# Storing full slots in 128 pieces of 16 KB instead of 256 pieces of 8 KB

## The chip, the cores and the metric

The kernel runs on one core of a Trainium2 chip. Times are microseconds on the device, from the first to the last thing that the program does there. Data come from the chip's main memory (HBM) into the on-chip memory (SBUF, 128 partitions) and go back by DMA; 16 DMA engines serve the core.

## The reference

There are 128 matrices `x[b]` of 128 x 1024 numbers (float32), eight weight matrices of 128 x 128, and one index per matrix.

```python
def _L0_cond_ref(x, subjects, weights):
    w = weights[subjects]
    out = jnp.einsum('bct,bcd->bdt', x, w)
    return out
x = x + _L0_cond_ref(x, itok_B_0_7, L0_cond_weights)
```

So every matrix is multiplied by the weight matrix that its index selects, and the product is added to it. Input and output are 67.1 MB each.

## The kernel before, in words

Four matrices (`H * G` = 2 x 2) make a slot: 16 KB in each of the 128 partitions, 2 MB in all. There are 32 slots of work (`NT`) and twelve places for them in SBUF (`SLOTS`); work slot i uses place i % 12. A half is two matrices (h = 0 or 1).

ScalarE's DMA queue issues the loads, one per matrix, 512 KB each (`load`, L137): 32 runs of 16 KB in HBM, four rows of the matrix to a run, into 4 KB in each of 128 partitions, one row to a partition. Slots 0 to 10 are loaded without a wait but for the weight copies that stand at slot 6 in ScalarE's program (L220 to L231); slot 11 waits until the weights have been turned (L233), since its place is used for that. From slot 12 on, ScalarE waits at L235 until slot i - 12 has been stored.

GpSimd waits for each slot's four loads (L240 to L244) and passes the word on to TensorE through `s_ready`. TensorE (`multiply`, L169) waits at L170 for the weights of the half, at L171 for the slot, and multiplies into PSUM at L175. VectorE (`add`, L184) waits for the product, adds it in place at L187 and copies the weights for the next slot (`place`, L164, L166).

SyncE's DMA queue loads the indices (L193) and the weight matrices, in 32 runs of 16 KB (L195), and then issues the stores (`store`, L145). It first waits until slot 7 has been loaded (L246, `AHEAD` = 8) and then, slot by slot, until the second half has been added (L250, `s_added`). Slots 0 to 30 are stored whole, by one DMA of 2 MB each: these are the full slots. Slot 31 is stored in a first half of 1 MB, then one matrix of 512 KB, then the last matrix by L279. When a store has landed, its place is free and ScalarE may issue the loads of the slot 12 further on. Nothing in this is decided by a scheduler: the order in each queue is the order of the code.

In SBUF a full slot is one run of 16 KB in each partition. In HBM its rows lie in four matrices, 4 KB in each. `store` cuts the SBUF side into pieces of `g` matrices:

```python
out[b + q0 : b + q1].rearrange("g d t -> d g t"),
xs[i % SLOTS][:, q0:q1, :].rearrange("d (o g) t -> d o (g t)", g=min(G, q1 - q0)),
```

Of the kernel before, what the change touches and what calls it, by code (L numbers as in the profile page):

```python
# [30 lines left out]
G = 2  # L31
# [4 lines left out]
SLOTS = 12  # L36
# [19 lines left out]
def transfer(nc, engine, out, in_):  # L56

    later, nc._always_lower_symbolic_ap = nc._always_lower_symbolic_ap, False  # L60
    ins, outs = engine.lower_ap_dma(in_), engine.lower_ap_dma(out)
    nc._always_lower_symbolic_ap = later
    return engine.add_instruction(
        mybir.InstDMACopy(
            name=nc.get_next_instruction_name(),
            engine=engine.engine,
            ins=ins,
            outs=outs,
            mode="Copy",
            cce_op=ALU.bypass,  # L70
            queue=QUEUES[engine.engine],
        )
    )
# [3 lines left out]
def kernel(  # L77
# [17 lines left out]
    if room:  # L95
        sbuf("room", C, room // 4)
    x_all = sbuf("x_all", C, SLOTS * H * G * T)
    xs = [
        x_all[:, i * H * G * T : (i + 1) * H * G * T].rearrange("c (q t) -> c q t", t=T)
        for i in range(SLOTS)  # L100
    ]
# [43 lines left out]
    def store(i, q0, q1):  # L145
        b = i * H * G
        transfer(
            nc,
            nc.sync,
            out[b + q0 : b + q1].rearrange("g d t -> d g t"),  # L150
            xs[i % SLOTS][:, q0:q1, :].rearrange("d (o g) t -> d o (g t)", g=min(G, q1 - q0)),
        ).then_inc(s_slot[i % SLOTS], DMA)

    def subjects_of(i):
# [36 lines left out]
    with tc.tile_critical():  # L191
# [55 lines left out]
        for i in range(NT):  # L247
            for h in range(H):
                if i == NT - 1 or h == H - 1:
                    nc.sync.wait_ge(s_added, i * H + h + 1)  # L250
                    store(i, h * G if i == NT - 1 else 0, (h + 1) * G - (i * H + h == NT * H - 1))
# [62 lines left out]
```

## Time and profile before

| | |
|---|---|
| median of 3 runs | 324.44 us (324.38 to 324.48) |
| the profiled execution | 323.93 us, its span 322.2 us |
| DMA | 134.76 MB in 15,059 packets, 418 GB/s over the span |
| PE busy | 239.5 us (74%) |
| VectorE busy | 168.2 us (52%) |
| stores of 2 MB | 31, median 44.9 us from issue to landing |
| loads of 512 KB | 128, median 10.6 us from issue to landing |

PE is TensorE's matmuls, DVE is VectorE, ACT ScalarE, POOL GpSimd, SP SyncE. q10 is ScalarE's DMA queue and q1 SyncE's. A DMA packet in these views is one piece of a transfer, or one of the small packets of 4 bytes that count a transfer's arrival, one per engine and transfer. A row of the windows gives the stretch, its length, busy time and instructions of PE, PE's weight loads, DVE, ACT and POOL, then the granted TensorE clock, the share of the 16 DMA engines and GB/s. A row of the waits gives who waited for whom: total, times, longest, in us.

### The profile page before, as it was taken

The page shows a single profiled execution, that of the slowest core. Times are in us where ns is not written, and L with a number is a line of the kernel's source. Part 1 is how long each engine was busy: PE and PEld are TensorE (multiplying, and loading weights), DVE is VectorE, ACT ScalarE, POOL GpSimd, SP SyncE. Part 2 cuts the span into 40 slices and gives each one's busy share as a digit, 9 for nine tenths or more (in the row PEclk, how much of TensorE's full clock was granted, in tenths as well). Part 3 has the DMA queues.
Part 4 walks back from the last instruction along what each step waited for, and adds up shares of the span by engine and source line. Part 5 has one row for each costly group of instructions (what it writes and reads, how often), then busy time and mean ns, then how long its engine had stood idle before and what let it go on. Part 6 is the DMA issues. An engine that isn't in the chain of part 4 may idle for free. (4 is left out here: it accounts for less than half of the span.)

```text
span 322.2 us, 2399 instructions
## 1 busy us (share of the span) xinstructions
PE 239.5 (74%) x518; PEld 99.4 (31%) x518; DVE 168.2 (52%) x204; ACT 11.1 (3%) x17; POOL 0.2 (0%) x4
## 2 busy tenths in 40 slices
PE   5001999999999999999999999996959779300000
PEld 2000344444444444444444444432423234000000
DVE  3002367767776776677677667763754707500000
ACT  0094000000000000000000000000000000000000
POOL 0000000000000000000000000000000000000000
PEclk9555799999999999999999999997998959755555
DMA  7999999999999999999999999999999999999996
GB/s 291 425 423 427 429 410 410 438 420 419 431 432 428 417 422 425 430 423 425 429 423 426 427 431 422 424 429 436 427 411 425 437 415 427 426 425 426 426 429 279
DMA packets 15059, 134.76 MB, mean 418 GB/s; under 512 B 2609, under 2 KB 2610, under 8 KB 2866
## 3 DMA queue, kind: packets, MB, share of 16 engines
q1 hardware_dynamic: 8914, 67.64, 49.9%
q10 hardware_dynamic: 6144, 67.12, 49.6%
q14 instruction: 1, 0.01, 0.0%
HBM read 67.63 MB, written 67.11 MB: 418 GB/s over the span
## 5 line engine op out<-in xcount | busy, mean ns | idle before, releaser
L175 PE MATMUL ps<-x_all,w 128*128 x512 | 234.8, 617 | 35.2 <-DVE w L166 24.6
L187 DVE TENSOR_TENSOR x_all<-ps,x_all 128x2048 f32 x64 | 146.7, 2292 | 84.6 <-DVEq L186 84.6
L175 PEld LDWEIGHTS ps<-x_all,w 128*128 128x128 f32 x512 | 97.6, 196 | 172.4 <-issue 171.5
L166 DVE COPY w<-w_runs 128x128 f32 x132 | 23.2, 219 | 0.8 <-DVE w_runs L262 0.8
L262 DVE STREAM_TRANSPOSE w_runs<-x_all 128x1024 f32<-128x1024 f32 x1 | 1.2, 1245 | 21.0 <-ACT x_all L224 21.0
L224 ACT COPY x_all<-x_all 32x256 f32<-32x256 f32 x16 | 9.8, 614 | 0.4
L205 PE MATMUL ps<-zeros 128*128 128x512 f32 x6 | 4.7, 952 | 1.7 <-DVE zeros L202 1.7
L205 PEld LDWEIGHTS ps<-zeros 128*128 128x128 f32 x6 | 1.8, 325 | 3.7 <-issue 2.1
L260 DVE STREAM_TRANSPOSE x_all<-w_runs 128x1024 f32<-128x1024 f32 x1 | 1.2, 1245 | 2.8 <-DMA w_runs<-in_L_cond_weights_dram 2.8
L224 ACT ACT_TABLE_LOAD x1 | 1.3, 1283 | 16.6 <-issue 16.6
L202 DVE MEMSET zeros<- 128x512 f32 x1 | 0.5, 485 | 1.0 <-SPq L191 1.0
L214 DVE TENSOR_SCALAR near<-given 1x128 int32<-1x128 int32 x1 | 0.2, 215 | 0.6 <-DMA given<-in_itok_B_dram 0.6
L218 DVE CUSTOM_DVE_ANT_0 index<-near,wrap 1x256 uint16<-1x256 uint16 x1 | 0.3, 278 | 0.0
L216 DVE TENSOR_SCALAR wrap<-near 1x128 int32<-1x128 int32 x1 | 0.2, 216 | 0.0
L301 POOL MEMSET const-bfloat16-1.0<- 128x1 bf16 x1 | 0.1, 101 | 0.0
L301 POOL MEMSET const-uint8-127<- 128x1 uint8 x1 | 0.1, 101 | 0.0
L301 POOL MEMSET const-float32-0.0<- 128x1 f32 x1 | 0.1, 98 | 0.2 <-issue 0.2
L301 POOL MEMSET const-float32-1.0<- 128x1 f32 x1 | 0.1, 98 | 0.0
L301 DVE BASE_LOAD x1 | 0.0, 21 | 0.1
L212 DVE MEMSET index<- 1x4 int32 x1 | 0.1, 62 | 0.0
## 6 DMA issues: line engine op xcount, KB each, us to landing
x_all<-in_x_dram ACTq DMA_DIRECT2D x128, 512.0 KB, 10.6
out_dram<-x_all SPq DMA_DIRECT2D x31, 2048.0 KB, 44.9
out_dram<-x_all SPq DMA_DIRECT2D x1, 1024.0 KB, 25.9
out_dram<-x_all SPq DMA_DIRECT2D x2, 512.0 KB, 21.2
w_runs<-in_L_cond_weights_dram SPq DMA_DIRECT2D x1, 512.0 KB, 4.4
given<-in_itok_B_dram SPq DMA_DIRECT2D x1, 0.5 KB
```

Source lines behind the costliest of these rows:

```text
L166: copy = nc.vector.tensor_copy(ws[q], w_all[:, bass.ds(subject[q], 1), :])
L175: mm = nc.tensor.matmul(ps[h][:, q % G, t : t + N], ws[q][:, 0, :], x_all[:, bass.ds(at, N)], start=True, stop=True,)
L187: nc.vector.tensor_tensor(mine, ps[h].rearrange("d g t -> d (g t)"), mine, ALU.add).then_inc(s_added, 1)
L202: nc.vector.memset(zeros, 0.0).then_inc(s_zeros, 1)
L205: nc.tensor.matmul(ps[P_SLOTS - 1][:, G - 1, :N], zeros[:, :D], zeros, start=True, stop=True)
L214: nc.vector.tensor_scalar(near, given, -S, S - 1, ALU.max, ALU.min).then_inc(s_index, 1)
L216: nc.vector.tensor_scalar(wrap, near, 0, S, ALU.is_lt, ALU.mult).then_inc(s_index, 1)
L218: nc.vector.tensor_tensor(index[:, :B], near, wrap, ALU.add).then_inc(s_index, 1)
L224: nc.scalar.copy(w_moved[b * BLOCK : (b + 1) * BLOCK, :].rearrange("l (a m h k j) -> l a h m k j", a=BLOCKS, m=PER, j=RUN, k=BLOCK // RUN) ...
L260: nc.vector.transpose(w_turned, w_runs).then_inc(s_wall, 1)
L262: nc.vector.transpose(w_runs, w_moved).then_inc(s_wall, 1)
L301: nc = _bacc.Bacc("TRN2", target_bir_lowering=False, num_devices=1)
```

## The change

Where a store covers four matrices, the SBUF side is handed over as one piece of 16 KB in each partition (`g` = 4) instead of two of 8 KB (`g` = 2). Stores of two matrices or of one keep their form. The bytes, the order of the code and all waits stay the same, and so do the instructions on every engine.

```diff
     def store(i, q0, q1):
         b = i * H * G
         transfer(
             nc,
             nc.sync,
             out[b + q0 : b + q1].rearrange("g d t -> d g t"),
-            xs[i % SLOTS][:, q0:q1, :].rearrange("d (o g) t -> d o (g t)", g=min(G, q1 - q0)),
+            xs[i % SLOTS][:, q0:q1, :].rearrange("d (o g) t -> d o (g t)", g=q1 - q0),
         ).then_inc(s_slot[i % SLOTS], DMA)
```

## The prediction, made before the changed kernel ran

> **What bounds the kernel now.** I read the page's strips first, then the windows, then the DMA view cut to two stretches, then the waits. In the page's strip the DMA engines are busy in every slice:
>
> ```profile
> DMA  7999999999999999999999999999999999999996
> DMA packets 15059, 134.76 MB, mean 418 GB/s; under 512 B 2609, under 2 KB 2610, under 8 KB 2866
> ...
> q1 hardware_dynamic: 8914, 67.64, 49.9%
> q10 hardware_dynamic: 6144, 67.12, 49.6%
> ```
>
> q10 is ScalarE's queue (128 loads), q1 SyncE's (stores, weights, indices). The two shares add to 99.5% of 16 engines' span, so the end is set by bytes over 427 GB/s. The packet counts are pieces plus 16 small count packets of 4 B for each DMA: a load is 32 pieces of 16 KB, on one engine two pieces and one count (128 x 48 = 6144); a full store is 256 pieces of 8 KB, on one engine sixteen and a count.
>
> The windows show what lies behind PE: it is done by 280 us, and 40 us of pure storing follow.
>
> ```profile
> 272.00:280.00 8.00, 4.36 (x11) 1.60 (x9) 5.23 (x7) 0.00 (x0) 0.00 (x0) 0.91 1.01 426
> 280.00:288.00 8.00, 0.00 (x0) 0.00 (x0) 0.00 (x0) 0.00 (x0) 0.00 (x0) 0.50 1.01 426
> ...
> 304.00:312.00 8.00, 0.00 (x0) 0.00 (x0) 0.00 (x0) 0.00 (x0) 0.00 (x0) 0.50 1.01 427
> ```
>
> So today the last slot's loading, matmuls and adds are covered by a backlog of some ten slots of stores. That cover is what the change touches. The DMA view for 50 to 100 us, where both queues hold work, shows how they share:
>
> ```profile
> q10 hardware_dynamic: 1136, 12.34, 58.3%
> q1 hardware_dynamic: 1162, 9.00, 42.6%
> ```
>
> Packet numbers are equal, bytes are not: an engine takes one packet from one queue, then one from the other. The trace's packet records of one engine read load, store, load, store, count, store, over and over. Last, who waits on PE:
>
> ```profile
> PE ps L175 <- PEq L171: 10.5, 3, 4.0
> ```
>
> PE lacked a loaded slot three times only (near 217, 236 and 256 us).
>
> **Part 1: fewer packets.** 31 stores lose 128 pieces each: 3968 packets, so q1 has 4946. In the packet records an 8 KB store piece takes 310.7 ns and a 16 KB load piece 616; 4 KB takes 159. The line through the store sizes gives 614 for 16 KB. Two small pieces cost 621.4, one large one 614 to 616: 5.4 to 7.4 ns saved 3968 times over 16 engines, 1.3 to 1.8 us. The other bound is the rate: loads alone run at 428 GB/s (10 to 40 us), stores alone at 426 (268 to 312), and half a per cent of the stores' 152 us is 0.7. I take 1.4, the packet price, because it is for the same byte count on the same engines. It counts only while the engines stay full.
>
> **Part 2: the shares.** Turns stay one for one, but a store turn now carries 16 KB. Before, the 17 turns of a store on an engine go with 17 load turns, 5.67 loads: 2.97 + 2.10 MB in 11.9 us, a loaded slot every 8.4 us. The trace confirms it: slots 9 to 12 are complete at 58.8, 67.1, 75.5 and 84.1 us. After, a store has 9 turns, beside 3 loads: 1.57 + 2.10 MB in 8.6 us. A slot is stored every 8.6 us and loaded every 11.5 us while both queues hold work.
>
> [...]
>
> **Part 3: where that leads.** All up to the first store packet at 48.6 us stays. PE and DVE take 7.05 us a slot (adds of one half start at 101.1 and 108.2), so slot i starts at 36 + 7.05 i as long as it is there. Slot 8 is there at about 50.5 and slot i at 50.5 + 11.5 (i - 8). These meet at slot 17, 158 us. From there PE waits at L171 for every slot, 4 us each; DVE, SP's waits for s_added and the stores behind them on SP follow.
>
> A slot's last add ends 10 us after its last load (0.35 to start, 7.05 matmuls, 2.3 add, small gaps), and about 2 us more pass before its store can move. Stores could begin at 48.6 + 8.6 i; the data are ready at 50.5 + 11.5 (i - 8) + 12. These meet at slot 27, about 280 us. Then the store queue runs dry, where before it held ten slots.
>
> How late is the last load? The engines are full until then. Most of them finish everything at 319.5 us before, so 318.1 with the 1.4 saved. A slot's store takes 4.87 us of all engines. If n slots have been stored when the last load ends, that is at 318.1 - 4.87 (32 - n). Slot 30 cannot be among them: it lands less than 12 us ahead of slot 31. Slot 29 is ready some 8 us ahead and takes its turns against the last loads. So n is between 29 and 30: 303.5 to 308.4 us. I take 29.8, 307.4, since a store with every second turn is through in 8.6 us.
>
> From there nothing covers the chain: landing 0.5, start 0.35, matmuls 7.05, add 2.3, issue 0.1, first packet about 2 (an uncontended first load needed 1.3, the first store under load 4.5), two 512 KB stores at 16 pieces x 159 ns = 2.5, end of program 1.4 (322.15 less 320.75). That is 16.2. If the clock drops, 1.7 more: after the waits at 217 and 236 us the next two slots took 15.88 us instead of 14.1, at a granted clock of 0.5 for 3.4 us. The wait ahead of slot 31 is 2 to 4 us, like those, so I count 1.4 of it. Span: 307.4 + 16.2 + 1.4 = 325.0.
>
> **Sum.** The profiled execution took 323.93 us, span 322.2 and 1.7 around it. New: 325.0 + 1.7 = 326.7, 2.8 more. The median of the runs shown is 324.44, 0.5 above the profiled one, so 327.2. Hidden at no cost: PE's waits in the middle (14 slots x 4 us), because the engines have queued loads throughout; if that cover failed each would show. The code's other orders, and DVE, ACT and POOL instructions, do not change.
>
> **Rivals.**
> First, *the chain stays covered*. If n is near 29, the last load ends at 303.5 and the chain without a clock drop at 319.7, when the engines are still busy with slot 30; then only the saving shows: 324.4 - 1.4 = 323.0. For it: 5 us, one slot's store, decide, and loads get every turn that a dry store queue leaves; it wins where the last load ends before 304.5. Against: slot 29 is ready too early to leave its turns unused. The same time comes out if turns are whole groups of pieces, so that the shares do not move: against it stand the equal packet numbers. Together 0.21. [...]
> Second, *cancelled*: last load near 305.5 without a drop, span within 0.6 us of today's: 324.4, chance 0.06.
> Third, *pieces are cut* on the way, at the 4 KB rows of the output, and nothing moves: 324.4. Against: loads with 4 KB rows on the on-chip side appear as 16 KB packets. Chance 0.03.
> Fourth, *worse*: stores of slot 30 also get in ahead of the last loads, or slot 31 meets two windows of half clock (one wait of 4.0 us before cost 2.9): last load at 309.5, chain 19.5, span 329: 331. Chance 0.09.
> My forecast keeps 0.61.
>
> **Numbers.** What a measurement of this kernel can tell from no change is about 0.2%, 0.65 us. Faster is the first rival, 0.21. Same: the second and third, 0.09. Slower: the forecast and the fourth, 0.70. The range goes from the covered case, 322.9, to 330.0, short of the fourth rival; the forecast's own range is 325.5 to 329.
>
> **What would show it.** q1 at 4946 packets; in the window 50 to 100 us equal packet numbers but about 8.5 MB loaded to 12.8 MB stored; slots loaded every 11.5 us; PE waiting at L171 from 160 us on some 14 times; last matmul near 316 instead of 276; DMA gaps and less than full rate in the last 10 us. It is wrong if loads keep 58%, if the last load ends before 304 us, or if 16 KB store pieces are far from 615 ns.

## The result, and the profile after

The changed kernel takes 326.08 us (median of 22 runs), the kernel before 324.10 us in runs beside it. The ratio is 1.0056, with a 95% interval of 1.0032 to 1.0079, about 1.8 us slower. One of the 22 runs, of 329.69 us, lies more than 1.5% above the shortest and is left out of the comparison. The kernel has also become uneven: 324.02 to 328.44 us over the other 21 runs, where nearly all runs of the kernel before lie between 323.6 and 324.7. The execution that was profiled is one of the long ones: 328.25 us, span 326.5.

The page of the changed kernel, the DMA strip, packets and queues:

```profile
DMA  7999999999999999999999999999999999999956
...
DMA packets 11091, 134.76 MB, mean 413 GB/s; under 512 B 2609, under 2 KB 2610, under 8 KB 2866
...
q10 hardware_dynamic: 6144, 67.12, 49.0%
q1 hardware_dynamic: 4946, 67.64, 48.8%
```

The 3968 packets are gone. What is new is the 5 in the strip's last slices: the engines run short of work near the end. The DMA view of the changed kernel for 50 to 100 us, the same stretch as before:

```profile
q1 hardware_dynamic: 829, 12.27, 57.7%
q10 hardware_dynamic: 838, 9.09, 43.0%
```

Packets are again one for one, and now the stores have the larger share of the bytes. So the loads fall behind. The timeline of PE in the changed kernel (start, time, instructions, and in brackets the idle time ahead and what ended it) shows the place, and the waits show its total:

```profile
154.98 7.13 PE L175 MATMUL ps<-x_all,w 128*128 x16 [0.64 <-PEq L171]
166.66 8.83 PE L175 MATMUL ps<-x_all,w 128*128 x16 [4.55 <-PEq L171]
178.32 7.13 PE L175 MATMUL ps<-x_all,w 128*128 x16 [2.84 <-DVE w L166]
...
298.28 7.13 PE L175 MATMUL ps<-x_all,w 128*128 x16 [1.51 <-PEq L171]
309.94 8.82 PE L175 MATMUL ps<-x_all,w 128*128 x16 [4.53 <-PEq L171]
```

```profile
PE ps L175 <- DVE w L166: 38.6, 6, 24.2
PE ps L175 <- PEq L171: 29.1, 10, 4.5
```

From 155 us on PE takes one slot at a time and then waits. Rows that name DVE's weight copy belong to the same wait: at 178 us the copy for that half had long been done (at 174.9 us), and GpSimd's record says that the slot was complete at 177.97 us. The row at 309.94 is the last slot. The last time in GpSimd's view of L244 is the moment at which slot 31 is complete. The kernel before, and below it the changed kernel, 42 us later:

```profile
L244 POOLq EVENT_SEMAPHORE  x31: 17/17/17, 14.6 to 267.5; - x31
```

```profile
L244 POOLq EVENT_SEMAPHORE  x31: 17/17/17, 14.7 to 309.6; - x31
```

What that does to the end is seen in the windows of the changed kernel (last two columns: DMA share and GB/s):

```profile
304.00:312.00 8.00, 3.47 (x7) 1.31 (x6) 3.40 (x6) 0.00 (x0) 0.00 (x0) 0.90 1.00 426
312.00:316.00 4.00, 4.00 (x8) 1.63 (x7) 0.36 (x1) 0.00 (x0) 0.00 (x0) 0.77 0.66 279
316.00:318.00 2.00, 2.00 (x6) 0.95 (x5) 2.00 (x3) 0.00 (x0) 0.00 (x0) 1.00 0.00 0
318.00:320.00 2.00, 0.77 (x2) 0.00 (x0) 1.19 (x3) 0.00 (x0) 0.00 (x0) 1.00 0.46 197
```

The store of slot 30 is through at 315.9 us by the packet records, and then the engines have nothing to do but wait for slot 31's matmuls and adds.

### The profile page after: what moved, and what is told of

It is laid out like the page before. It is cut to its first block, busy times and chain, and to the rows that moved or that the text cites. A ratio compares the mean times of both kernels' runs of the same rounds, so it can differ in the third digit from the quotient of the medians.

```text
span 326.5 us, 2399 instructions
## 1 busy us (share of the span) xinstructions
PE 249.4 (76%) x518; PEld 102.7 (31%) x518; DVE 168.2 (52%) x204; ACT 11.1 (3%) x17; POOL 0.2 (0%) x4
## 3 DMA queue, kind: packets, MB, share of 16 engines
q1 hardware_dynamic: 4946, 67.64, 48.8%
## 5 line engine op out<-in xcount | busy, mean ns | idle before, releaser
L175 PE MATMUL ps<-x_all,w 128*128 x512 | 244.1, 635 | 67.7 <-DVE w L166 38.6
L175 PEld LDWEIGHTS ps<-x_all,w 128*128 128x128 f32 x512 | 100.8, 202 | 211.6 <-issue 211.0
L166 DVE COPY w<-w_runs 128x128 f32 x132 | 23.2, 218 | 0.8 <-DVE w_runs L262 0.8
## 6 DMA issues: line engine op xcount, KB each, us to landing
x_all<-in_x_dram ACTq DMA_DIRECT2D x128, 512.0 KB, 40.3
out_dram<-x_all SPq DMA_DIRECT2D x31, 2048.0 KB, 25.6
```

Of the source, the lines that this page charges most:

```text
L166: copy = nc.vector.tensor_copy(ws[q], w_all[:, bass.ds(subject[q], 1), :])
L175: mm = nc.tensor.matmul(ps[h][:, q % G, t : t + N], ws[q][:, 0, :], x_all[:, bass.ds(at, N)], start=True, stop=True,)
```

## The experiments

The theory is the one of the prediction: the engines take one piece from each queue in turn, as the 829 packets beside 838 above have it, so a piece's size sets its queue's share; with 16 KB store pieces the loads come late, and past a certain point the last slot's chain (load, matmuls, add, store) has no stores left to hide behind. The rival is that a 16 KB store piece is itself what costs. "Last slot" in the table further down is GpSimd's record of the moment at which slot 31 is complete. Each edit is shown against the changed kernel; e3 makes its edit in the kernel before.

**e5: the same pieces, with a head start for the loads.**

```diff
-AHEAD = 8
+AHEAD = 10
```

> The changed kernel, with its first store let go when slot 9 is loaded instead of slot 7 (AHEAD = 10); pieces as in the changed kernel. Turns theory: loads start the shared part two slots further ahead and the stores some 10 us later, the last slot is loaded near 302 us and is covered or nearly so: within 1.5 us below or 0.5 above the kernel before, 322.8 to 324.6. Rival (the piece itself costs): stays near 326.

324.00 us against 323.90, ratio 1.0004 (0.9995 to 1.0013). All 31 full stores have 16 KB pieces and q1 has 57.7% of the engines' time between 60 and 110 us, as in the changed kernel, yet nothing is lost. PE's last slot begins at 303 us, and the windows of e5 show the engines at full rate until the usual end:

```profile
q1 hardware_dynamic: 845, 12.27, 57.7%
```

```profile
303.37 8.56 PE L175 MATMUL ps<-x_all,w 128*128 x16 [2.66 <-PEq L171]
```

```profile
312.00:318.00 6.00, 0.00 (x0) 0.00 (x0) 2.56 (x3) 0.00 (x0) 0.00 (x0) 0.88 0.97 409
```

PE waits nearly as long in e5 as in the changed kernel (28.8 us at L171 and 33.1 put down to L166, beside 29.1 and 38.6). So neither the piece nor PE's waits cost anything by themselves that these runs can tell. The rival falls here.

**e8: half that head start.**

```diff
-AHEAD = 8
+AHEAD = 9
```

> The changed kernel with AHEAD = 9: its first store waits for slot 8 instead of slot 7, half as much as the run with AHEAD = 10. Turns theory: what decides is whether the store of slot 29 or 30 still moves ahead of the last load; with this start the phase falls on the late side, the last slot is loaded near 308 to 309.5 us and the end is 2.5 to 4.5 us above the kernel before, 326.4 to 328.4. Rival (a head start of the loads is worth the same for each slot): half of what AHEAD = 10 gives back, near 325.

327.08 us against 323.75, ratio 1.0087 (1.0068 to 1.0105): a slot more of head start makes it no better than the changed kernel, as the turns theory had it, by which the stores that still move ahead of the last load decide. In the packet records, store pieces worth 29.7 slots have begun in e8 when the last load ends, as in the changed kernel's first execution, and 28.5 in e5. The rival asked for 325 us. The last slot is complete at 309.55 us.

```profile
309.90 8.82 PE L175 MATMUL ps<-x_all,w 128*128 x16 [2.07 <-PEq L171]
```

**e2 and e7: the large pieces early only, or late only.**

```diff
-            xs[i % SLOTS][:, q0:q1, :].rearrange("d (o g) t -> d o (g t)", g=q1 - q0),
+            xs[i % SLOTS][:, q0:q1, :].rearrange("d (o g) t -> d o (g t)", g=q1 - q0 if i < 24 else min(G, q1 - q0)),   # e2
+            xs[i % SLOTS][:, q0:q1, :].rearrange("d (o g) t -> d o (g t)", g=q1 - q0 if i >= 8 else min(G, q1 - q0)),   # e7
```

> 16 KB pieces for the stores of slots 0 to 23 only, 8 KB from slot 24 on. Turns theory: loads run at 40% until the stores of slot 24 move (near 255 us) and get 57% from there, the last slot is loaded near 299 us, ten us sooner, and the chain behind it is covered: 0 to 1 us below the kernel before, 323.2 to 324.2. Rival (the piece itself costs): 24 of 31 stores still have the large pieces, so three quarters of the loss stay, near 325.5.

> 8 KB pieces for the stores of slots 0 to 7, 16 KB from slot 8 on. Turns theory: the early stores leave the loads their 57%, the last slot is loaded near 291 us, the end is covered. What is left is the price of the packets: 23 stores save 2944 records, by 5.6 ns each less the 3 ns by which records overlap 0.5 us; and if the stall when stores set in (1.1 to 1.2 us in the traces of the changed kernel, 0.6 before) goes with the size of the first pieces, it is 0.6 again: 0.2 to 0.6 us below the kernel before. If the packets save nothing: level with it. Rival (the piece itself costs): two thirds of the loss, near 325.4.

e2: 324.05 against 323.90, ratio 1.0001 (0.9992 to 1.0010), last slot at 299.0 us. e7: 323.74 against 323.75, ratio 0.9996 (0.9988 to 1.0005), last slot at 292.2 us. In both the loss is gone, though three quarters of the stores have large pieces. But what was expected of the packets is gone too: with 3072 and 2944 packets fewer, both are level with the kernel before, within 0.1%.

**e4: small pieces.** All stores are cut into 4 KB, the full ones and slot 31's first half: 8064 packets more than before.

```diff
-            xs[i % SLOTS][:, q0:q1, :].rearrange("d (o g) t -> d o (g t)", g=q1 - q0),
+            xs[i % SLOTS][:, q0:q1, :].rearrange("d (o g) t -> d o (g t)", g=1),
```

> Full stores in 512 pieces of 4 KB. Turns theory: loads get 73%, the end stays covered, 7936 more packets cost 2 to 3.6 us by their records (twice 159 ns for 310.7, with or without the 3 ns by which records overlap): 326.1 to 327.7, last load near 268 us. Rival (smaller pieces suit the stores): not slower than the kernel before.

324.58 against 323.90, ratio 1.0019 (1.0008 to 1.0030). The loads were not held up, with a median of 7.5 us from issue to landing between 50 and 100 us (13.7 before), and the last slot is complete at 268.5 us. By an estimate from those 7.5 us their queue was not full throughout, and over that stretch they had 57.0% of the engines' time, not the 73% told. But the kernel lost 0.6 us, not 2 to 3.6. The expectation was not far off for the stores alone: from start to start of the packet records, where stores move alone, a full store keeps an engine busy 4.975 us in 4 KB pieces and 4.918 in 8 KB, 1.8 us more over 31 stores. It left out that the loads gain: between 100 and 250 us the next record on an engine begins 608 ns after a load piece where it was 613 before, which gives back an estimated 0.8 us over the loads that move beside stores.

**e6: the loads in small pieces beside the large stores.** 64 runs of 8 KB, with the stores of the changed kernel.

```diff
-            x[i * H * G + q].rearrange("(a r) t -> a (r t)", r=ROWS),
+            x[i * H * G + q].rearrange("(a r) t -> a (r t)", r=ROWS // 2),
```

> Stores in 16 KB pieces, loads in 64 runs of 8 KB instead of 32 of 16 KB. Turns theory: a load has five turns for 32 KB, loads get 31%, PE waits from about slot 12 on, the last slot is loaded near 305 to 311 us: 1 to 7 us above the kernel before, 325 to 331. Rival (the piece itself costs): only 4096 more packets than the changed kernel, 0.6 to 1.3 us above it, and PE waits as there.

326.97 against 323.90, ratio 1.0103 (1.0080 to 1.0126). By the time alone either theory would do, since the rival asked for 326.7 to 327.4. The loads' share falls as the turns have it, again at equal packet numbers; the DMA view of e6 for 50 to 100 us:

```profile
q1 hardware_dynamic: 1009, 14.70, 69.1%
q10 hardware_dynamic: 1009, 6.66, 31.8%
```

The last slot is complete at 312.0 us, 1 us beyond what was told, and PE's first long wait ends at 131 us, ahead of slot 13 and not of slot 17 as in the changed kernel. The rival had PE wait as in the changed kernel.

**e1 and e3: the loads in large pieces.** 16 runs of 32 KB, e1 with 16 KB stores and e3 with 8 KB.

```diff
-            x[i * H * G + q].rearrange("(a r) t -> a (r t)", r=ROWS),
+            x[i * H * G + q].rearrange("(a r) t -> a (r t)", r=2 * ROWS),
```

> Stores in 16 KB pieces as in the changed kernel, loads in 16 runs of 32 KB instead of 32 of 16 KB (the weights stay as they were). Turns theory (the engines take one piece from each queue in turn, so the size of a piece sets a queue's share, late loads leave the last slot's chain without cover): a load is two turns for 32 KB, a store nine for 128 KB, loads get 53% again, the last slot is loaded near 268 us, the end is covered, and only the saved packets show: 0.6 to 2 us below the kernel before, 322.3 to 323.5. Rival (a 16 KB store piece is itself what costs, by its reading or its four rows in HBM): no change from the changed kernel, near 326.

> Stores as before in 8 KB pieces, loads in 32 KB runs. Both theories: the loads' share rises from 57 to 68%, the last slot is loaded near 268 us as before because places limit it, and 2048 fewer packets save 0.3 to 0.9 us: 323.2 to 323.9. It prices the packets alone and is the other half of e1.

e1: 369.34 (median of the four runs compared; 370.71 of all seven) against 323.90, ratio 1.139 (1.136 to 1.143). e3: 391.88 (two compared; 396.06 of all six), ratio 1.209 (1.204 to 1.215). Both theories were far out, and for the question these two runs say little: loads in 32 KB pieces are slow beside either size of store. e1's trace is of one of the longer runs, 383.39 us. While it only loads, between 10 and 40 us, its DMA view reads:

```profile
DMA  9039099099099097091090390390390390590990
...
DMA packets 444, 7.28 MB, mean 243 GB/s; under 512 B 222, under 2 KB 222, under 8 KB 222
```

The shares are as the turns have them (between 100 and 200 us of e1, 1309 load packets beside 1310 store packets, 21.43 MB beside 19.10); the rate is not: 405 GB/s in that stretch, against 427 in the changed kernel from 100 to 260 us.

**Two more executions of the changed kernel.**

> The changed kernel again, for its trace. Turns theory: the time follows the end of the last load: the later it lands, the later the end, one for one above some 304 us, plus 1.7 us where the clock drops ahead of the last slot. Rival (piece): the time does not depend on it.

> As the run before it: a third trace of the changed kernel, same expectations.

325.10 and 326.63 us. Together with the others they give the relation that settles the matter, all in us (e1 and e3, whose loads are slow throughout, are left out):

| kernel | last slot complete | span |
|---|---|---|
| before | 267.5 | 322.2 |
| e4, 4 KB stores | 268.5 | 322.7 |
| e7, large pieces from slot 8 | 292.2 | 322.5 |
| e2, large pieces to slot 23 | 299.0 | 322.2 |
| e5, AHEAD 10 | 303.0 | 321.9 |
| changed kernel, second execution | 306.7 | 323.3 |
| changed kernel, third execution | 308.0 | 324.9 |
| e8, AHEAD 9 | 309.6 | 326.4 |
| changed kernel, first execution | 309.6 | 326.5 |
| e6, 8 KB loads | 312.0 | 327.8 |

Up to 303 us the last slot's moment makes no difference, over 35 us. From 306.7 on the span follows it: 16.6, 16.9, 16.9 and 16.9 us behind in the changed kernel and e8, 15.8 in e6. The knee, where 322.2 less 16.7 puts it, is at about 305.5.

## Why the prediction was right, and what was mis-sized

**Part 2** held. 829 and 838 packets for equal turns, and 9.09 MB loaded beside 12.27 stored where 8.5 and 12.8 were told. Slots 9 to 13 are complete at 63.1, 74.8, 85.8, 97.5 and 109.2 us: 11.5 us apart.

**Part 3** held in its steps. PE first lacks a slot at 155 us (158 told), at slot 17. It then mostly waits 2 to 4.6 us a slot, and these waits cost nothing, as e5 shows by having nearly all of them. The store queue runs dry: the median from issue to landing falls from 44.9 us to 25.6 for a full store, and for a load it rises from 10.6 to 40.3. In the packet records no store piece moves from 282.0 to 284.9 us and from 293.0 to 295.2. The chain was put at 17.6 us from the end of the load data, with 0.5 of that for the landing, so 17.1 from the landing; it measures 16.6 to 16.9. Its terms moved a little: matmuls 8.82 us in the first execution, where the granted clock is 0.5 for 3.4 us from 310.5 us on, as told, and the last matrix's store is issued 1.2 us after the last add (321.30 to 322.53 us) and not 0.1.

**Part 1** is the term that was mis-sized: 1.4 us told, and none seen within 0.1%, that is 0.3 us. The packet record is what was forecast (615.8 ns for a 16 KB store piece, told 614 to 616; 621.4 for two of 8 KB). But a record begins 3 to 4 ns before the end of the one ahead of it on its engine, which the sum did not take off. From start to start, where stores move alone, two 8 KB pieces take 614.0 ns (kernel before) and one of 16 KB takes 612.8 to 612.9 (e5, e7); a full store keeps an engine busy 4.918 us in 8 KB pieces and 4.908 to 4.910 in 16 KB. That leaves 0.3 us over 31 stores, too little to be told from nothing here. The other bound, from the rates, had said 0.7 and was nearer. (By the same records a store's 4.87 us in Part 3 is 4.92, 0.1 us in the sum.)

In these two traces more than that goes where the stores set in. The windows of the kernel before and, below it, of the changed kernel, 40 to 50 us:

```profile
40.00:50.00 10.00, 10.00 (x24) 4.07 (x23) 7.26 (x9) 0.00 (x0) 0.00 (x0) 1.00 0.99 394
```

```profile
40.00:50.00 10.00, 10.00 (x24) 4.13 (x23) 7.25 (x10) 0.00 (x0) 0.00 (x0) 1.00 1.00 376
```

18 GB/s less over 10 us is 0.18 MB, or 0.4 us at 427 GB/s. It does not go with the size of the pieces. From 40 to 56 us e7, which begins with 8 KB pieces, moves 394 GB/s, no more than the changed kernel's 396; e2, which begins with 16 KB pieces, moves 410, like the kernel before (411). What sets it is open.

**The last load** was put at 307.4 us, 307.9 with its landing, from 29.8 stores moved by then. Three executions have its data through at 308.5, 306.3 and 306.9 us and the slot complete at 309.6, 306.7 and 308.0. Store pieces worth 29.74, 29.27 and 29.37 slots had begun by then; put into the sum of Part 3 with the end at 319.5, without the 1.4 saved, they give 308.5, 306.2 and 306.7. So the step was right; 29.8 was a little high, and the saving that did not come made up for it.

**The sum** was 327.2, the median is 326.08. That they lie so close is in part luck: without the saving the same sum gives 328.6, the time of the longest executions, and the median is lower because other executions end earlier. Forecast and first rival are not two cases of which one holds; by the times both occur. Six of the 21 runs lie at 324.0 to 324.3, like covered ones, and without a saving they come out level with the kernel before and not at 323.0; none of these six was traced. The others spread up to 328.4. Why the same kernel ends early in one execution and late in the next was not settled. GpSimd's records place part of it: slot 28 is complete at 281.3 us in the first and in the third execution, slot 31 at 309.6 and 308.0, so these two part only in the last 30 us or so, where the store queue runs dry (from 282.0 us on in the first, from 291.9 in the third).

The second rival's time, near 324.4, thus has more weight than it was given. The third (pieces cut on the way) is ruled out by 4946 packets. The fourth asked for 331, and no run came there; its 2.9 us for a long wait is 2.7 by its row (16.83 less 14.1). The first rival's other way to its time, turns of whole groups of pieces, would keep the shares only if a turn took all of a store's records on an engine, 17 before and 9 after; with any fixed number of pieces to a turn the shares would move as with one. The packet records of the changed kernel show one piece a turn: from 50 to 100 us, wherever the next record on the engine can be told, all 308 load pieces are followed by a record of the stores and all 409 store pieces by one of the loads. The shares moved from 12.34 MB loaded against 9.00 stored to 9.09 against 12.27.

## What to carry to other kernels

Where two DMA queues compete, look at their packet numbers in a stretch where both are full. In the kernel before (1136 of the loads beside 1162 of the stores), the changed kernel (838 beside 829), e1 (1309 beside 1310) and e6 (1009 beside 1009) they were equal but for 2%, so that the size of a piece set the queue's share, and larger pieces on one side slowed the other side though no byte was added: 9.09 MB loaded in 50 us and not 12.34. With the DMA engines full, late loads cost this kernel nothing where the last slot was complete by 303.0 us (spans of 321.9 to 322.7 us); from 306.7 us on its own chain, 15.8 to 16.9 us, was longer than the stores that were left, and the span went up, to 327.8 us. So work out that moment and keep clear of it. Fewer packets were worth little here: 3968 fewer are worth 0.3 us by their records, too little to be seen in the time, and 8064 more, in 4 KB pieces, cost 0.6.

## What the runs showed that was not expected

Load runs of 32 KB, one to each engine and DMA, were far slower than two of 16 KB. While nothing else moves, a piece takes 2176 ns in e1's packet records where two pieces of 16 KB take 1232, and the loads run at 243 GB/s instead of 428. Beside stores, from 100 to 200 us, nearly three quarters of the 32 KB pieces take less than 1300 ns, most of the others up to some 1750. What makes them slow was not tried.

The time does not go steadily with the head start: AHEAD at 8, 9 and 10 gives ratios of 1.0056, 1.0087 and 1.0004. The turns theory told e8's time ahead, as a matter of which stores fall before the last load, but no run follows that step by step.
